# Node rows loaded before the branch, layer 1's weights prepared in the experts' stage, and its entry done tile by tile

## The chip, the cores and the metric

The kernel runs on one core of a Trainium2 chip. The metric is the device time of one execution in microseconds (us), as the median of several runs. The engines of the core are TensorE (PE; its weight loads are shown apart as PEld), VectorE (DVE), ScalarE (ACT), GpSimd (POOL) and SyncE (SP). SP, ScalarE and GpSimd issue DMAs here; GpSimd issues the indirect ones, which fetch one row of a table per partition.

## The reference

A graph of N = 3125 nodes with D = 256 features and E = 50000 edges sorted by their target goes through two layers, each with a graph part, a mixer over all nodes and a feed-forward part of 8 experts. Everything is float32. Cut to its outline:

```python
xn = layernorm(x)
x = x + gnn0(xn, edges, edge_attr) + mixer0(xn)   # edge attention with 4 heads; 4 blocks of linear attention and an MLP
x = x + experts_top2(layernorm(x))                # each node goes to 2 of 8 experts, 256-512-256 with gelu
xn = layernorm(x)
x = x + gnn1(xn, edges) + mixer1(xn)              # layer 1
x = x + experts_all(layernorm(x))                 # all 8 experts, weighted by a softmax router
```

Of layer 1 the change touches the entry and the keys and values:

```python
# gnn1: mean of the neighbours' rows, then [xn, mean] @ weight, each row divided by its norm, plus bias
# mixer1:
k, v = split(xn @ w_qkv + b_qkv)                  # 8 heads of 32
k = layernorm(k) * kln_g + kln_b                  # within a head
v = layernorm(v) * vln_g + vln_b
kv = sum over nodes of k^T v / N                  # one 32 x 32 context per head
h = gelu((q @ kv + xn) @ w1 + b1)
mixer1 = h @ w2 + b2 + xn
```

## The kernel before

`gps_kernel` (L116) turns the list of targets into columns (`edge_columns`, L155), compares them with the windows that the kernel was laid out for, reads the resulting flag into a register and branches: `fast_path` (L188) if the edges lie inside the windows, else `general_path`, which does not run here. The nodes stand in 25 tiles of Q = 128 rows (NT = 25, the last with 53), in one SBUF tensor X that is updated in place. The edges stand in 391 blocks of 128.

Layer 0 begins in `fast_path`. SP issues six loads of X (L369, groups of five tiles), then the source list, then the weights of the graph part (L373 to L383); the table loop (L384 to L397) normalises each tile (`ln_stats` L255, `normed` L267), transposes it (`transposed` L270), multiplies it (`product` L277) and stores the rows that the edge gathers read. `mixer` (L530) begins with statistics of the already normed rows (`stats_of`, L532), one pair of VectorE instructions for each tile. Edge work and mixer work are interleaved by a planner that compares costs and due times. `dispatch` (L794) routes each node to two experts and scatters its row to the `tok` table.

The experts' stage (L893 to L1012) runs 32 tiles of 256 rows. For each, SP loads rows and weights three tiles ahead (`load(k + 3)`), TensorE does two products with a Gelu on ScalarE between them, and the result is stored to the table `yex` by ScalarE's queue. Behind tile 8, 11, 14 and so on SP also loads the weights of layer 1's experts.

Then comes layer 1. Its weights are loaded and prepared at L1025 to L1050: six loads on SP, six rows spread over the partitions on ScalarE's queue, the mean of each head taken out of the key and value weights on VectorE, the query weight transposed. The entry loop (L1053 to L1079) goes through chunks of four tiles: `yex` rows are gathered (two for each tile, GpSimd) and added to X with their gates (L1064), the rows are normed by VectorE (L268), transposed into xT, multiplied by the node half of the graph weight and stored into the table `xtab`, from which the edge gathers of layer 1 read. The normed rows and the bias are then added to X:

```python
        nc.vector.tensor_tensor(xs, xs, xn[:, 0:n, :], ALU.add)
        nc.vector.tensor_tensor(xs, xs, bc(gb, 1, n), ALU.add)
```

After the entry, `other()` runs `mixer1` (L1101) and then `experts` (L1193), whose steps yield an estimate of their time; a loop (L1305 to L1315) puts a group of eight edge blocks (`sum_group`, L1270) in whenever enough of that time has been spent:

```python
    spent, g, PACE, FROM = 0.0, 0, 11.5, 14.0
        while g < len(GROUPS) and (step is None or spent >= FROM + PACE * g):
```

A group's rows are fetched by GpSimd into one of three buffers `gt1`, three groups ahead. `mixer1` takes one step for each tile for keys and values: product (two inputs of 512 columns), bias and norm within a head, then scale and shift by lng and lnb over the whole tile (L1118, L1119), then two context products that add up in PSUM over all 25 tiles; each such step yields 3.7. With the context closed, it is folded into the first MLP weight, and the MLP runs over groups of tiles from the top (`BACK`, L1098: six groups of four and a last one of tile 0 alone). `experts` takes the same groups: a group's router (`route`, L1167) and experts run when its edge sums are all in and `aggregate` (L1235) has added them to X. In PSUM there are the kinds "seg", "tr", "mm" and "acc" with two buffers each. The order of instructions on an engine follows the order of the program; where the loops above put a step decides what it queues behind.

## Time and profile before

| what | value |
|---|---|
| median of three runs | 2773.26 us (2771.87 to 2775.46) |
| profiled execution | 2773.55 us |
| its span | 2771.8 us |
| granted TensorE clock, mean | 0.968 |
| PE busy | 2596.2 us (94%) |
| PEld busy | 1875.5 us (68%) |
| DVE busy | 1523.5 us (55%) |
| ACT busy | 870.6 us (31%) |
| POOL busy | 932.1 us (34%) |
| moved by DMA | 215.84 MB |

The profile is of one execution; its span runs from the first to the last instruction. A row of digits cuts the span into 40 slices of 69.3 us; a digit is the busy share in tenths, and PEclk is the granted clock of TensorE in tenths. A window line gives a stretch, then the engines' busy time in it with the number of instructions. A line of the chain gives start, length, and the engine, PSUM kind and source line. "L280" is the product helper, so that products are told apart by the name of what they write.

### The profile page before, as it was taken

What the parts mean: (1) busy time and instruction counts of PE and PEld (TensorE: products, weight loads), DVE (VectorE), ACT (ScalarE), POOL (GpSimd) and SP (SyncE); (2) the same over time, 40 slices, a digit from 0 to 9 for tenths busy, and PEclk for the clock granted to TensorE, in tenths of its full rate; (3) what the DMA queues carried; (4) which work ended last, traced back from release to release, by engine and by line L of the source; (5) the groups of instructions that cost most, each with busy time, mean ns of one, the idle gap of its engine ahead of it and who ended that gap; (6) DMA issues with size and microseconds to landing.
All of it is one profiled execution on the core that took longest, in us unless ns stands there. A gap on an engine that the chain in (4) does not pass through costs nothing.

```text
span 2771.8 us, 29883 instructions
## 1 busy us (share of the span) xinstructions
PE 2596.2 (94%) x10578; PEld 1875.5 (68%) x10578; DVE 1523.5 (55%) x3754; ACT 870.6 (31%) x1619; POOL 932.1 (34%) x962
## 2 busy tenths in 40 slices
PE   5989999899898999898998899678899999999998
PEld 4866778667677667685666788545666666666655
DVE  6576666866668777678654311389644333232211
ACT  3432235322253222533332222232333232222233
POOL 1208552154531544200222000267555454545100
PEclk9999999999999999999997899889999999999999
DMA  4103331032212131101210886443222222222000
GB/s 146 24 14 94 86 107 30 21 90 77 88 53 75 43 87 37 56 3 38 63 51 34 263 268 209 156 121 93 67 71 76 70 69 74 82 65 77 19 8 11
DMA packets 152337, 215.84 MB, mean 78 GB/s; under 512 B 21033, under 2 KB 120687, under 8 KB 152179
## 3 DMA queue, kind: packets, MB, share of 16 engines
q1 hardware_dynamic: 104274, 112.31, 12.7%
q0 software_dynamic: 36848, 91.34, 12.0%
q10 hardware_dynamic: 11056, 10.19, 1.1%
q8 instruction: 86, 1.41, 0.2%
q14 instruction: 73, 0.59, 0.1%
HBM read 160.14 MB, written 53.61 MB: 77 GB/s over the span
## 4 chain that ended last, share of the span: by engine, by line
PE 83%; DVE 10%; ACT 2%; DMA 2%; issue 2%; POOL 1%; SPq 0%; DVEq 0%; ACTq 0%; POOLq 0%
PE mm L280 35%; PE acc L280 26%; PE seg L467 6%; PE seg L1280 6%; PE acc L614 3%; PE tr L274 3%; PE acc L335 1%; POOL gt L283 1%; PE seg L280 1%; DVE gt L422 1%; DVE kv L1116 1%; DMA ye<-yex,slot 1%; PE tr L280 1%; PE tr L982 1%; DVE kv L1118 0%
## 5 line engine op out<-in xcount | busy, mean ns | idle before, releaser
L283 POOL DMA_INDIRECT gt<-table,srcI x391 | 439.3, 1124 | 690.3 <-DVE m L425 496.5
L283 POOL DMA_INDIRECT gt<-xtab,srcI x391 | 385.2, 985 | 351.5 <-PE seg L1280 205.6
L280 PE MATMUL mm<-hT,w 128*128 128x512 f32 (+2 forms) x896 | 372.6, 555 | 10.1 <-ACT gT L690 8.6
L280 PE MATMUL acc<-w,gT 128*128 128x256 f32 x1600 | 366.8, 384 | 0.0
L280 PEld LDWEIGHTS acc<-w,gT 128*128 128x128 f32 x1600 | 302.5, 192 | 45.1 <-issue 2.5
L1221 ACT ACTIVATE fh<-mm,bn_b,bn_s 128x512 f32<-128x512 f32 (+1 forms) x224 | 163.1, 731 | 431.7 <-PE mm L280 431.7
L339 DVE SCALAR_TENSOR_TENSOR X<-acc,rw,X 128x256 f32<-128x256 f32 x200 | 95.2, 483 | 324.8 <-PE acc L280 324.5
L280 PEld LDWEIGHTS mm<-hT,w 128*128 128x128 f32 x896 | 164.1, 192 | 142.9 <-issue 93.7
L690 ACT ACTIVATE gT<-mm,cols 128x512 f32<-128x512 f32 (+2 forms) x224 | 142.2, 641 | 352.1 <-PE mm L280 351.7
L280 PE MATMUL mm<-wqkv,hT 128*128 128x256 f32 x800 | 210.0, 393 | 9.2 <-ACT K L566 6.3
L280 PE MATMUL acc<-fw_f_Wo,fh 128*128 128x256 f32 x800 | 198.1, 385 | 1.0
L280 PE MATMUL mm<-fh,fw_f_W 128*128 128x512 f32 (+1 forms) x448 | 197.0, 569 | 1.6 <-ACT fh L1221 1.3
L280 PE MATMUL mm<-xc,fw_f_W 128*128 128x512 f32 (+1 forms) x448 | 189.3, 552 | 0.0
L467 PE MATMUL seg<-vals,oh 128*128 128x261 f32 x782 | 184.0, 387 | 3.7 <-DVE vals L457 3.7
L1280 PE MATMUL seg<-gt,oh 128*128 128x256 f32 x782 | 184.3, 385 | 0.0
L280 PEld LDWEIGHTS acc<-fw_f_Wo,fh 128*128 128x128 f32 x800 | 144.7, 190 | 58.1 <-issue 18.5
L467 PEld LDWEIGHTS seg<-vals,oh 128*128 128x128 f32 x782 | 147.8, 191 | 38.0 <-DVE oh L290 5.4
L1280 PEld LDWEIGHTS seg<-gt,oh 128*128 128x128 f32 x782 | 149.5, 193 | 33.3 <-issue 13.0
L280 PEld LDWEIGHTS mm<-wqkv,hT 128*128 128x128 f32 x800 | 142.5, 195 | 32.7 <-ACT K L566 10.7
L280 PEld LDWEIGHTS mm<-fh,fw_f_W 128*128 128x128 f32 x448 | 78.8, 192 | 100.7 <-issue 65.4
L1059 POOL DMA_INDIRECT ye<-yex,slot x50 | 52.2, 1044 | 264.1 <-DVE bn_b L1092 249.2
L701 DVE TENSOR_TENSOR X<-acc,X 128x256 f32<-128x256 f32 x100 | 42.2, 422 | 151.9 <-PE acc L280 151.7
(333 smaller groups left out, 3864.5 us busy)
## 6 DMA issues: line engine op xcount, KB each, us to landing
ew<-in_e_W SPq DMA_DIRECT2D x64, 512.0 KB, 6.9
tok<-zero SPq DMA_DIRECT2D x8, 3328.0 KB, 12.7
w<-in_W SPq DMA_DIRECT2D x8, 1024.0 KB
hr<-tok SPq DMA_DIRECT2D x32, 256.0 KB, 4.7
yex<-yo ACTq DMA_DIRECT2D x32, 256.0 KB, 5.0
gt<-table,srcI POOLq DMA_INDIRECT x391, 2.6
gt<-xtab,srcI POOLq DMA_INDIRECT x391, 2.7
fw_f_W<-in_f_W SPq DMA_DIRECT2D x16, 256.0 KB, 4.0
```

Source lines behind the costliest of these rows:

```text
L274: nc.tensor.transpose(pt[:, k, :], src_row[:, k * Q:(k + 1) * Q], ident)
L280: nc.tensor.matmul(pm, a, b, start=(k == 0), stop=(k == len(lhs) - 1))
L283: nc.gpsimd.indirect_dma_start(out=dst, out_offset=None, in_=tab[:, :], in_offset=bass.IndirectOffsetOnAxis(ap=srcI[:, b:b + 1], axis=0))
L335: nc.tensor.matmul(py, cT[:, j, :], bt, start=True, stop=True)
L339: nc.vector.scalar_tensor_tensor(X[:, t, :], py, cw, X[:, t, :], op0=ALU.mult, op1=ALU.add)
L467: nc.tensor.matmul(open_seg[w_], oh[:, b - h0, :], v[:, b - h0, :], start=(b == a), stop=(b == z))
L614: nc.tensor.matmul(cx[a], K[0:r, t, a * 128:(a + 1) * 128], keys.hn[0:r, t, :], start=(t == 0), stop=(t == NT - 1))
L690: nc.scalar.activation(gT[:, f, :], pm, AF.Gelu, bias=col("b1", l * NF + f))
L701: nc.vector.tensor_tensor(X[:, t, :], py, X[:, t, :], ALU.add)
L1059: nc.gpsimd.indirect_dma_start(out=ye[0:r, j, :], out_offset=None, in_=yex[:, :], in_offset=bass.IndirectOffsetOnAxis(ap=slot[0:r, k, t0 + ...
L1221: nc.scalar.activation(hn[:, a, 0:w], pm, AF.Relu, bias=bn[s][1][:, c:c + 1], scale=bn[s][0][:, c:c + 1])
L1280: nc.tensor.matmul(segs[w], oh[:, j, :], gt[:, j, :], start=(b == z), stop=(b == a))
```

## The change

X is allocated ahead of the branch, and its six loads go onto SP directly behind the load of the target list; `node_dma` becomes a function of the module. The statistics that open `mixer` are taken from those of the table loop, as variance times the squared factor of the norm, with a mean of zero.

A generator `layer1_weights` loads and prepares layer 1's weights in five parts, called behind tiles 9, 12, 15, 18 and 21 of the experts' stage. New in it are four masks `cf` made of lng and lnb: the scale and shift of keys and values are no longer done on the rows, but on the finished context. For that a column of ones is kept beside each 128 of the normed keys and values, the context products get 129 columns, and one more product with a matrix of ones gives column sums of 258 columns, held in a "seg" buffer over all tiles.

The entry is rewritten tile by tile. Rows are fetched by `fetch_y` in groups of 2, 3, 4, 4, 4, 4 and 4 tiles into the three `gt1` buffers; `add_y` adds them and takes statistics four tiles ahead; `norm_y` writes the normed row on ScalarE and, in place of adding it, scales X by one plus the factor; `product_y` is the node product and its store. Steps of `keys_values` are put between the tiles, about three for four tiles; those left over (of 28) run in `mixer1` and yield 2.5 each. The bias add moves to `mixer1`'s loop over `BACK`, whose groups become four of four and three of three tiles. The expert norms are computed behind the entry.

```diff
+    X = pre.tile([Q, NT, D], F32, name="X", tag="X")
...
+        nc.gpsimd.memset(X[:, NT - 1, :], 0.0)
+        for t0, n in TG:
+            node_dma(nc.sync, X[:, t0:t0 + n, :], i["x"], t0, n)
...
-        fast_path(tc, i, out, ident, dstP)
+        fast_path(tc, i, out, ident, dstP, X)
...
-            for t0, n in TG:
-                node_dma(nc.sync, X[:, t0:t0 + n, :], i["x"], t0, n)
...
+                v = mv1[:, t0:t0 + n, 1]
+                nc.vector.tensor_tensor(v, mv[:, 0:n, 1], rs[:, 0:n], ALU.mult)
+                nc.vector.tensor_tensor(v, v, rs[:, 0:n], ALU.mult)
...
-            for t in range(NT):
-                stats_of(mv1, t)
...
+    def layer1_weights():
+
+        w = {}
+        w["qkv"] = weights("m_wqkv", 3 * D)
+        w["kvb"] = row_load(lp, "kv_b")
+        lng = row_load(lp, "kvln_g").rearrange("p (s d) -> p s d", s=2)
+        lnb = row_load(lp, "kvln_b").rearrange("p (s d) -> p s d", s=2)
+        yield w
+        w["1"] = weights("m_w1", D)
+        w["2"] = weights("m_w2", D)
+        w["gb"] = row_load(lp, "g_bias")
+        mb2 = row_load(lp, "m_b2")
+        w["br"] = row_load(lp, "br")
+        yield w
+        w["g"] = weights("g_w", D, 2 * KC)
+        w["r"] = weights("f_Wr", NE)
+        w["fbo"] = lp.tile([NE, D], F32, name="fbo", tag="fbo")
+        nc.sync.dma_start(w["fbo"], i["f_bo"])
+
+        hm = lp.tile([Q, KC + 1, 2 * NH], F32, name="hm", tag="hm")
+        for k in range(KC + 1):
+            v = (w["qkv"][:, k, D:3 * D] if k < KC else w["kvb"]).rearrange("p (h d) -> p h d", d=DH)
+            nc.vector.tensor_reduce(hm[:, k, :], v, AX.X, ALU.add)
+            nc.vector.tensor_scalar(hm[:, k, :], hm[:, k, :], 1.0 / DH, None, op0=ALU.mult)
+            nc.vector.tensor_tensor(v, v, bc(hm[:, k, :], 2, DH), ALU.subtract)
+        yield w
+        nc.vector.tensor_tensor(w["gb"], w["gb"], mb2, ALU.add)
+
+        w["qT"] = lp.tile([Q, KC, D], F32, name="wqT", tag="wqT")
+        for k in range(KC):
+            pt = transposed(w["qkv"][:, k, 0:D])
+            nc.vector.tensor_copy(w["qT"][:, :, k * Q:(k + 1) * Q], pt)
+        yield w
+
+
+        four = lp.tile([Q, 2, Q], F32, name="four", tag="four")
+        vc = lp.tile([Q, 2], F32, name="vcol", tag="vcol")
+        for s, row in enumerate((lng, lnb)):
+            nc.vector.tensor_copy(four[:, s, :].rearrange("p (h d) -> p h d", d=DH), bc(row[:, 1, :], 1, Q // DH))
+            pt = ps("tr", [Q, Q])
+            nc.tensor.transpose(pt, four[:, s, :], ident)
+            nc.vector.tensor_copy(vc[:, s:s + 1], pt[:, 0:1])
+        w["cf"] = lp.tile([Q, 4, Q], F32, name="cf", tag="cf")
+        nc.vector.memset(w["cf"], 0.0)
+        for s in range(2):
+            for j in range(Q // DH):
+                r = slice(j * DH, (j + 1) * DH)
+                nc.vector.tensor_scalar(w["cf"][r, 2 * s, r], (lng, lnb)[s][r, 0, :], 1.0 / N, None, op0=ALU.mult)
+            nc.vector.tensor_scalar(w["cf"][:, 2 * s + 1, :], w["cf"][:, 2 * s, :], vc[:, 1:2], float((1, N)[s]),
+                                    op0=ALU.mult, op1=ALU.mult)
+            nc.vector.tensor_scalar(w["cf"][:, 2 * s, :], w["cf"][:, 2 * s, :], vc[:, 0:1], None, op0=ALU.mult)
+        yield w
+
+    l1w, ready = None, layer1_weights()
...
+            if k >= 9 and k % 3 == 0:
+                l1w = next(ready, l1w)
...
-    BACK = [list(range(t, max(-1, t - 4), -1)) for t in range(NT - 1, -1, -4)]
+    BACK = [list(range(t, t - 4, -1)) for t in range(NT - 1, 8, -4)] + [list(range(t, t - 3, -1)) for t in (8, 5, 2)]
...
-        for j in range(n):
-            normed(xn[:, j, :], xs[:, j, :], mv, rs, j)
...
-        nc.vector.tensor_tensor(xs, xs, xn[:, 0:n, :], ALU.add)
-        nc.vector.tensor_tensor(xs, xs, bc(gb, 1, n), ALU.add)
...
+    ENT = [(0, 2), (2, 3)] + [(t, 4) for t in range(5, NT, 4)]
...
+    def fetch_y(g):
+        if g < len(ENT):
+            t0, n = ENT[g]
+            yes[g] = wk.tile([Q, 8, D], F32, name="ye", tag="gt1", bufs=3)
             for j in range(n):
                 r = rows(t0 + j)
+                for k in range(2):
+                    nc.gpsimd.indirect_dma_start(
+                        out=yes[g][0:r, 2 * j + k, :], out_offset=None, in_=yex[:, :],
+                        in_offset=bass.IndirectOffsetOnAxis(ap=slot[0:r, k, t0 + j:t0 + j + 1], axis=0))
+
+    def add_y(t):
+
+        g = ENT_OF[t]
+        t0, n = ENT[g]
+        r = rows(t)
+        for k in range(2):
+            nc.vector.scalar_tensor_tensor(X[0:r, t, :], yes[g][0:r, 2 * (t - t0) + k, :], gate[0:r, k, t:t + 1],
+                                           X[0:r, t, :], op0=ALU.mult, op1=ALU.add)
+        st = stat.tile([Q, 6], F32, name="st", tag="st", bufs=4)
+        nc.vector.bn_stats(st, X[:, t, :])
+        nc.vector.bn_aggr(mvx[:, t, :], st)
+        if t == t0 + n - 1:
+            a, b, c = (rsx[:, k, t0:t0 + n] for k in range(3))
+            nc.scalar.activation(a, mvx[:, t0:t0 + n, 1], AF.Sqrt, bias=eps5)
+            nc.vector.reciprocal(a, a)
+            nc.vector.scalar_tensor_tensor(b, mvx[:, t0:t0 + n, 0], -1.0, a, op0=ALU.mult, op1=ALU.mult)
+            nc.vector.tensor_scalar(c, a, 1.0, None, op0=ALU.add)
+            fetch_y(g + 3)
+
+    def norm_y(t):
+
+        xn = wk.tile([Q, D], F32, name="xn", tag="h", bufs=2)
+        nc.scalar.activation(xn, X[:, t, :], AF.Identity, scale=rsx[:, 0, t:t + 1], bias=rsx[:, 1, t:t + 1])
+        pt = transposed(xn)
+        nc.scalar.copy(xT[:, :, t, :], pt)
+        nc.scalar.activation(X[:, t, :], X[:, t, :], AF.Identity, scale=rsx[:, 2, t:t + 1], bias=rsx[:, 1, t:t + 1])
+
+    def product_y(t):
+        t0, n = ENT[ENT_OF[t]]
+        if t == t0:
+            yts[t0] = c4("yt").rearrange("p a (b c) -> p (a b) c", c=D)
+        py = ps("seg", [Q, D])
+        product(py, [xT[:, k, t, :] for k in range(KC)], [l1w["g"][:, KC + k, :] for k in range(KC)])
+        nc.scalar.copy(yts[t0][:, t - t0, :], py)
+        if t == t0 + n - 1:
+            nc.sync.dma_start(xtab[t0 * Q:(t0 + n) * Q, :].rearrange("(t p) c -> p t c", p=Q), yts.pop(t0)[:, 0:n, :])
+
+    def keys_values():
+
+        cx = [ps("acc", [Q, Q + 1]) for _ in range(2)]
+        ks = ps("seg", [Q, 2, Q + 1])
+
+        def sums(t):
+            kv, r = kvs[t % 3], rows(t)
+            se = dict(start=(t == 0), stop=(t == NT - 1))
+            for a in range(2):
+                nc.tensor.matmul(cx[a], kv[0:r, 2 + a, 0:Q], kv[0:r, a, :], **se)
+            nc.tensor.matmul(ks.rearrange("p a c -> p (a c)"), ones[0:r, :], kv[0:r, 0:2, :].rearrange("p a c -> p (a c)"),
+                             **se)
+
+        for t in range(NT + 2):
+            if t < NT:
+                pm = ps("mm", [Q, 2 * D])
+                product(pm, [xT[:, k, t, :] for k in range(KC)], [l1w["qkv"][:, k, D:3 * D] for k in range(KC)])
+                ks_ = c4("kv").rearrange("p s (h d) -> p s h d", d=DH)
+                kv, sq = ks_[:, 0], ks_[:, 1]
+                nc.vector.tensor_tensor(kv.rearrange("p h d -> p (h d)"), pm, l1w["kvb"], ALU.add)
+                nc.scalar.activation(sq, kv, AF.Square)
+                va = wk.tile([Q, 2 * NH], F32, name="va", tag="va")
+                nc.vector.tensor_reduce(va, sq, AX.X, ALU.add)
+                nc.scalar.activation(va, va, AF.Sqrt, bias=eps5, scale=1.0 / DH)
+                nc.vector.reciprocal(va, va)
+                nc.vector.tensor_tensor(kvs[t % 3][:, :, 0:Q].rearrange("p g (h d) -> p g h d", d=DH),
+                                        kv.rearrange("p (g h) d -> p g h d", g=4),
+                                        bc(va, 2, DH).rearrange("p (g h) d -> p g h d", g=4), ALU.mult)
+            if t >= 2:
+                sums(t - 2)
+            yield
+        cb = lp.tile([Q, 2, Q], F32, name="cb1", tag="four")
+        c2 = lp.tile([Q, Q], F32, name="cb2", tag="cb2")
+        sv = lp.tile([Q, 2], F32, name="sumv", tag="sumv")
+        cf = l1w["cf"]
+        for a in range(2):
+            nc.vector.tensor_copy(sv[:, a:a + 1], cx[a][:, Q:Q + 1])
+            nc.vector.tensor_tensor(cb[:, a, :], cx[a][:, 0:Q], cf[:, 0, :], ALU.mult)
+            nc.vector.scalar_tensor_tensor(cb[:, a, :], cf[:, 2, :], sv[:, a:a + 1], cb[:, a, :],
+                                           op0=ALU.mult, op1=ALU.add)
+            nc.vector.tensor_tensor(c2, ks[:, a, 0:Q], cf[:, 1, :], ALU.mult)
+            nc.vector.tensor_tensor(cb[:, a, :], cb[:, a, :], c2, ALU.add)
+            nc.vector.tensor_tensor(cb[:, a, :], cb[:, a, :], cf[:, 3, :], ALU.add)
+        contexts.append(cb)
...
+    contexts = []
+    for g in range(3):
+        fetch_y(g)
+    AHEAD = 4
+    for t in range(AHEAD):
+        add_y(t)
+    norm_y(0)
+    kvsteps, due = keys_values(), 0
+    for t in range(NT):
+        if t + AHEAD < NT:
+            add_y(t + AHEAD)
+        if t + 1 < NT:
+            norm_y(t + 1)
+        product_y(t)
+        while due < 0.75 * t - 0.5:
+            next(kvsteps)
+            due += 1
+    norms_of_experts()
...
-            nc.vector.tensor_tensor(k4, k4, bc(lng, 2, NH), ALU.mult)
-            nc.vector.tensor_tensor(k4, k4, bc(lnb, 2, NH), ALU.add)
...
-            yield 3.7
...
+        for _ in kvsteps:
+            yield 2.5
+        cb = contexts[0]
...
+            nc.vector.tensor_tensor(X[:, t0:t0 + n, :], X[:, t0:t0 + n, :], bc(l1w["gb"], 1, n), ALU.add)
...
```

## The prediction

> **What bounds the kernel now.** I read the slices first, then windows by stage, then the waits and the chain of the one stretch that stands out. The slices of the page:
>
> ```profile
> PE   5989999899898999898998899678899999999998
> PEclk9999999999999999999997899889999999999999
> DMA  4103331032212131101210886443222222222000
> ```
>
> TensorE is at 9 or 10 tenths nearly everywhere, so only its gaps and its own work count. The gaps are slice 1, slices 22 to 23 and slices 26 to 29. The windows (PE, PEld, DVE, ACT, POOL busy; granted clock; DMA share; GB/s) say how large the last is:
>
> ```profile
> 1540.00:1773.70 233.70, 233.67 (x1137) 203.59 (x1136) 45.41 (x70) 59.62 (x126) 0.00 (x0) 1.00 0.72 229
> 1600.00:1640.00 40.00, 40.00 (x197) 34.95 (x196) 7.60 (x11) 10.40 (x22) 0.00 (x0) 1.00 0.92 298
> 1773.70:1957.90 184.20, 127.57 (x433) 82.93 (x433) 157.45 (x349) 48.29 (x120) 110.54 (x106) 0.82 0.36 108
> 2000.00:2200.00 200.00, 198.06 (x724) 131.48 (x723) 83.40 (x195) 64.25 (x105) 105.11 (x108) 0.98 0.26 74
> ```
>
> The experts' stage (first row) is all TensorE, with VectorE and ScalarE mostly free. Layer 1's entry and its keys and values (third row) are VectorE's: 157 of 184 us, TensorE at clock 0.82. From 2000 TensorE rules again. In the chain TensorE's own pace is plain:
>
> ```profile
> 2419.05 4.29 PE mm L280 x10
> 2430.78 3.45 PE seg L1280 x16
> ```
>
> A 512-column instruction takes 0.429 us, one of 256 columns 0.2156, so one of 128 about 0.108. At this pace the third row's work is: keys and values products 100 x 0.429 = 42.9, node products 100 x 0.2156 = 21.6, contexts 100 x 0.108 = 10.8, edge sums 66 x 0.2156 = 14.2, aggregates 2.6, transposes 54 x 0.108 = 5.8: 98 us. The stretch lasts 184.2, so **86 us are lost there**: the pot. Its waits (who, for whom: us, times, longest) and two lines of the time line:
>
> ```profile
> PE tr L274 <- DVE xn L268: 26.3, 6, 11.6
> PE acc L1122 <- DVE kv L1119: 15.9, 10, 3.6
> DVE X L1064 <- DMA ye<-yex,slot: 8.3, 5, 6.2
> 1784.63 0.88 DVE L1064 SCALAR_TENSOR_TENSOR X<-ye,gate,X 128x256 f32<-128x256 f32 x2 [6.23 <-DMA ye<-yex,slot]
> 1859.96 1.46 POOL L283 DMA_INDIRECT gt<-xtab,srcI  x1 [15.43 <-DMA xtab<-yt]
> ```
>
> First TensorE waits for VectorE's normed rows, then for its normed keys and values; the edge gathers begin at 1860. The start shows in the chain:
>
> ```profile
> 10.13 4.81 DMA X<-in_x
> ...
> 17.01 10.01 DMA raw<-in_src
> ...
> 30.64 4.90 PE mm L280 x20
> ```
>
> The table's product waits until 30.6 for what SP issues behind the node rows.
>
> **The change, part by part.** The sum is made against the profiled run, 2773.55 us (its span 2771.8); the runs' median is 2773.26, the same for this purpose.
>
> *Node rows ahead of the branch.* Six loads on SP, 6.84 us of issue, move from 10.13 to about 1.3. SP sat there 7.9 us waiting for the flag, so the issue fits into that wait. They are put behind the dst load on SP and beside ScalarE's three small dst loads; should these land later the flag slips, at most about 1 us. Src, attention and table weights then meet DMA queues that are nearly empty of rows: they should come some 8.8 us earlier (10.13 - 1.3), and with them the product of 30.6, the table, the first gathers and layer 0, which has no slack. Bounds: 0, if something else gates the product, and -10; if the branch waits for outstanding loads (no row shows it), rows still come ahead of weights and about 5 stays. Taken: **-8.5**.
>
> *First statistics from the table's* (50 VectorE instructions, 25 x (0.38 + 0.16) = 13.5 us, between 39.8 and 52.1). They end at 52.1; the first normed row runs at 57.86, after the table's store. Nothing.
>
> *Weights in the experts' stage.* Six SP loads and six broadcast rows on ScalarE's queue, about 2.4 MB, go past the experts' own loads. VectorE gets 3 x (0.68 + 0.17 + 0.68) for the means and about 4 us more, beside 45 busy of 234. TensorE gets six transposes, 0.65 us, in a row with no idle. ScalarE's issues cost 0.47 us each (they did at 1777) ahead of a Gelu; TensorE has two "mm" buffers and waits for Gelu at once: at most 6 x 0.47 = 2.8. Here a rule speaks against the change: the Trainium skill, "DMA: Bandwidth & Descriptors", Specifications, gives some 358 GB/s of HBM bandwidth to a core. The row 1600 to 1640 already moves 298 at share 0.92. By the rule 60 are free and 2.4 MB need 40 us, which is hidden; if they all stood ahead of expert weights, 2.4 MB / 298 GB/s = 8 us. From 1640 the trace moves about 210 only, so I take nothing for bandwidth and **+3** in all (0 to 10).
>
> *Entry.* Removed from VectorE: two affine passes over keys and values (16.8 + 17.2), the residual adds (7.4 + 0.4; the bias add of 7.7 goes to the later feed-forward, where VectorE is 40% busy), the normed rows (9.2, to ScalarE), the weight preparation (5), the experts' norms (1.5). Left on VectorE up to the context: rows' sums and statistics 25 x (0.85 + 0.38 + 0.16) + 7 x 0.5 = 38; keys and values 16.6 + 16.5 + 6.1 + 17.0 = 56; context 3; six one-hots and five bucket sums 10: 107. The first sum no longer stands beside 2 MB of weights: gather at 1777.4, 1.56 to issue, landing as in the later gathers 2.6 after the issue began: 1780.5. In 1790 to 1850 VectorE was busy 87 to 100%; at 92% the 107 take 117: end at **1897**.
>
> TensorE: four gathers at 1.25, landing, sums, statistics, norm: first product about 1788. Work to the context 42.9 + 21.6 + 10.8 + 5.4, two groups' sums 6.9, aggregates 1.7, and new: the column sums, 50 instructions of 258 columns, **10.9**. Together 100: 1888 at best, so VectorE ends last. ScalarE: two normalising passes at 0.51 (its scaled copy L1240), two copies at 0.37, and (0.63 + 0.31) for keys and values: 2.7 x 25 = 68, hidden. POOL: 50 row gathers at 1.25 end at 1840; last row, product and store put the edge gathers at 1856 to 1866, as now. With folding the context and G about 5 us are bare: TensorE is saturated from 1902. Of 128.3 us since 1773.7 it worked 103.5; lost 25 instead of 86. Gain 86 - 25 - 10.9 = **-50**.
>
> A second rule: column sums hold one of the two "seg" buffers, so each node product waits for ScalarE's copy of the one before. The Trainium skill, "TensorE: Matmul & The Clock Gate", section on psum-queue depth-cycling, warns that micro-idles between matmul groups let the clock fall to half. By it, 100 us of work at the 0.83 of 1810 to 1840 would take 120, end 1908, gain 39. But those rows have TensorE busy only 6.4 of 10; now 2.6 us of keys-and-values work stands ready between two products, while a copy takes 0.37. I keep -50 and put 39 in the range.
>
> *Node order at the end.* The one-tile group ran 29.1 us (2737.3 to 2766.4) for 20.7 of work; a three-tile group should lose about 0.5 per expert, like a four-tile one: -4.4. But mixer units shrink from 25 x 3.7 to 10 x 2.5, so the last edge group (due at 14 + 48 x 11.5 = 566) comes just before the last tiles' experts (at 570), and their router can't be issued ahead: aggregate 4.1 + router 2.7, less 3 of other work; the last store is three tiles, +0.9. **+1** net (-4 to +6).
>
> Sum: 2773.5 - 8.5 + 3 - 50 + 1 = **2719**.
>
> **Rivals.** *A, half the pot* (0.22): keys and values are pushed behind the entry by its own VectorE work. Entry to 1852, then 56 + 3 + 16 at 92% = 82: 1934 instead of 1952, and the column sums are hidden: some -26. 2773.5 - 8.5 + 3 - 26 + 1 = 2743. For it: VectorE is at 9.4 to 10 from 1790 to 1820. Against: 25 us less of it per entry.
>
> *B, slower* (0.07): the waits that now stand at 1781, where ScalarE waits 10.2 us for a row load and TensorE 9.2 for a weight, move into the queues of the experts' stage and stop TensorE. Five points at 10.2 are 51; from 55 us on it decides: 2719 + 58 = 2777. Against: loads land in about 5 us there.
>
> *C, the rows bring nothing* (0.10): the branch drains them and the flag waits: 2728.
>
> *D, both engines full from 1790* (0.11): VectorE at 100% and keys and values all inside the entry: 1888, lost 15: 2706.
>
> **How the numbers follow.** The main case has 0.50, A 0.22, D 0.11, C 0.10, B 0.07. The range takes D and most of A, and the unknown bounds (experts' stage 0 to 10, clock 11): 2698 to 2745. Main, A, D and C are faster by over 0.2% (5.5 us, about what a measurement tells): 0.93. Of B, 0.03 only eats the gain up and stays within; 0.04 goes beyond: slower.
>
> **What would show it.** Table product at about 22 instead of 30.6; experts' stage 234 to 240 us long; first row sum at 1780.5 on the old clock (shifted by the start); VectorE about 107 busy to the context, which is closed about 123 us after the experts' end instead of 178; edge gathers still some 85 us after it; the last sums close to the last tiles' router. Wrong it would be if TensorE showed idle in the experts' stage, if VectorE stayed the last to end well after 1910, or if POOL made edge groups wait.

## The result, and the profile after

The changed kernel takes **2738.54 us** (median of four runs, 2737.68 to 2742.77) against 2772.57 for the kernel before (four runs): a ratio of 0.9878, 95% interval 0.9861 to 0.9896, so 34 us less. The forecast was 2719 with a range of 2698 to 2745: the direction and the range hold, but of the 54 us that were forecast 34 came. The profiled execution has a span of 2737.1 us at a mean clock of 0.975.

The slices of the page of the changed kernel (40 of 68.4 us):

```profile
PE   6989999899899999998998799969999999999998
PEclk9999999999999999999999799989999999999999
DMA  5003331032312131100111786542222222222200
```

Of the gap of slices 26 to 29 one slice is left, the 27th, with 6 tenths; slice 1 has risen from 5 to 6.

Windows by stage (columns as before: PE, PEld, DVE, ACT, POOL busy; granted clock; DMA share; GB/s). First the kernel before, from the end of the experts' stage to the first MLP product of layer 1, and ten microseconds near its beginning:

```profile
1773.70:1977.00 203.30, 146.49 (x523) 99.32 (x523) 173.28 (x390) 53.95 (x136) 121.37 (x117) 0.84 0.35 104
1780.00:1790.00 10.00, 1.08 (x4) 0.71 (x4) 5.37 (x14) 1.79 (x3) 7.56 (x9) 0.50 1.00 320
```

Then the changed kernel: its experts' stage, the same stretch behind it, and the beginning of that stretch in tens:

```profile
1541.72:1775.20 233.48, 231.58 (x1127) 201.37 (x1125) 46.83 (x79) 59.08 (x125) 0.00 (x0) 1.00 0.71 229
1775.20:1918.35 143.15, 111.30 (x462) 74.64 (x461) 103.08 (x257) 67.22 (x165) 76.77 (x76) 0.90 0.31 92
1780.00:1790.00 10.00, 0.00 (x0) 0.00 (x0) 3.89 (x11) 0.29 (x1) 7.56 (x9) 0.50 0.32 92
1790.00:1800.00 10.00, 3.25 (x8) 1.74 (x8) 4.73 (x16) 2.80 (x7) 7.57 (x9) 0.50 0.37 107
1800.00:1810.00 10.00, 7.92 (x25) 5.24 (x26) 6.57 (x24) 4.75 (x11) 7.56 (x9) 0.69 0.44 131
```

The stretch lasts 143 us instead of 203, with VectorE busy 103 instead of 173. What is left is its front. TensorE was nearly idle there before too (its first transposed row came 21.9 us behind the stage, now 19.9), but then it waited for a weight, and VectorE was full from 1790. Now TensorE does nothing at all from 1780 to 1790, and VectorE is not the reason by its load (39 and 47%). The waits of the changed kernel from 1770 to 2000 (who, for whom: us, times, longest), and from its time line the first product of the table and the first edge gathers of the two layers:

```profile
POOL gt L288 <- DVE va L1190: 40.0, 2, 39.7
...
PE tr L279 <- ACT xn L1153: 24.3, 3, 19.9
...
DVE X L1137 <- DMA ye<-yex,slot: 20.2, 23, 2.7
...
PE seg L285 <- ACT yt L1164: 5.6, 3, 3.4
```

```profile
23.33 2.18 PE L285 MATMUL mm<-wcat,xt 128*128 128x136 f32 x8
...
53.17 1.12 POOL L288 DMA_INDIRECT gt<-table,srcI  x1 [40.85 <-DVE hn L722]
...
1884.65 0.96 POOL L288 DMA_INDIRECT gt<-xtab,srcI  x1 [39.72 <-DVE va L1190]
```

TensorE's waits for keys and values (15.9 us before) are gone, and of those for normed rows one long one is left, 19.9 us. The product of the table comes 7.3 us earlier, layer 1's edge gathers 24.7 us later. The name in their wait (`va`) misleads: what they need is the last rows of `xtab`, whose product ended at 1880.3 and whose store was issued at 1880.7.

For the sum by stages, each TensorE instruction is counted at full pace (columns x 0.429 / 512 us, at least 0.108), and what a stretch lasts beyond that is called lost: idle time and slow clock together.

| stretch | before: length, lost | after: length, lost |
|---|---|---|
| start to the first output product of the experts' stage | 1542.4, 198.3 | 1541.7, 196.8 |
| experts' stage | 231.3, 2.1 | 233.5, 4.5 |
| its end to the first MLP product | 203.3, 87.2 | 143.1, 39.7 |
| from there to the end | 794.8, 49.9 | 818.7, 50.8 |

Behind the experts' stage the work at full pace went from 861.0 to 871.3 us. So the 34.7 us of the two spans are: start -0.7, experts' stage +2.2, lost time of the entry -47.4, work added +10.3, lost time behind it +0.9. These are one profile of each kernel. In the repeat of the changed kernel below, the entry lost 42.5 and the rest 54.9, so a term is known to some 4 us.

### The profile page after: what moved, and what is told of

It is laid out like the page before. It is cut to its first block, busy times and chain, and to the rows that moved or that the text cites. A ratio compares the mean times of both kernels' runs of the same rounds, so it can differ in the third digit from the quotient of the medians.

```text
span 2737.1 us, 29869 instructions
## 1 busy us (share of the span) xinstructions
PE 2581.4 (94%) x10630; PEld 1879.5 (69%) x10630; DVE 1475.2 (54%) x3670; ACT 892.3 (33%) x1668; POOL 934.7 (34%) x962
## 5 line engine op out<-in xcount | busy, mean ns | idle before, releaser
L285 PE MATMUL mm<-hT,w 128*128 128x512 f32 (+2 forms) x896 | 374.2, 557 | 10.3 <-ACT gT L694 8.8
L1388 PEld LDWEIGHTS seg<-gt,oh 128*128 128x128 f32 x782 | 147.6, 190 | 32.8 <-issue 11.5
L285 PEld LDWEIGHTS mm<-wqkv,hT 128*128 128x128 f32 x800 | 143.2, 196 | 33.2 <-ACT K L570 10.9
L285 PEld LDWEIGHTS mm<-xc,fw_f_W 128*128 128x128 f32 x448 | 85.9, 192 | 58.5 <-issue 40.5
```

What stands on the lines that cost most here:

```text
L285: nc.tensor.matmul(pm, a, b, start=(k == 0), stop=(k == len(lhs) - 1))
L1388: nc.tensor.matmul(segs[w], oh[:, j, :], gt[:, j, :], start=(b == z), stop=(b == a))
```

## The experiments

The experiments ran on three chips. On the first the kernel before takes 2772 us, on the two others 2952 and 2949. There TensorE, VectorE and ScalarE stand still together again and again, often with no wait that the profile shows (the last section has the numbers). Each run is therefore compared with others of its chip, and small differences on the slower chips stay open.

**The changed kernel again**, beside three of the other runs on the faster chip:

> The changed kernel once more, unchanged, as the measure for the others on this chip: its ratio to the kernel before should be near 0.988.

2744.74 us, ratio 0.9894 (0.9877 to 0.9910). Its MLP begins 145.9 us behind the experts' stage (143.1 in the first profile).

**The order on VectorE.** In the changed kernel the front of the entry reads like this in the time line (start, length, engine, line, operation, tiles; in brackets the idle time before it and what ended it):

```profile
1782.46 0.48 DVE L1137 SCALAR_TENSOR_TENSOR X<-ye,gate,X 128x256 f32<-128x256 f32 x1 [2.67 <-DMA ye<-yex,slot]
...
1789.36 0.29 ACT L1144 ACTIVATE rsx<-mvx,eps 128x2 f32<-128x2 f32 x1 [11.69 <-DVE mvx L1141]
...
1791.33 0.48 DVE L1137 SCALAR_TENSOR_TENSOR X<-ye,gate,X 128x256 f32<-128x256 f32 x1 [0.54 <-DMA ye<-yex,slot]
...
1792.57 0.48 DVE L1137 SCALAR_TENSOR_TENSOR X<-ye,gate,X 128x256 f32<-128x256 f32 x1 [0.67 <-DMA ye<-yex,slot]
...
1793.31 0.15 DVE L1145 RECIPROCAL rsx<-rsx 128x2 f32<-128x2 f32 x1
...
1794.46 1.09 ACT L1153 ACTIVATE xn<-X,rsx 128x256 f32<-128x256 f32 x2 [4.80 <-DVE mvx L1141]
...
1795.12 1.18 PE L279 MATMUL tr<-ident,xn 128*128 128x128 f32 x4 [19.89 <-ACT xn L1153]
```

ScalarE has the root of the first group's variances ready at 1789.65. The reciprocal that makes the factor of it needs 0.15 us, but on VectorE it stands behind row sums of later tiles, which wait for their gathered rows; it runs at 1793.31. The statistics that the root needs stood behind such sums too. The program text does not show this order: in it `add_y(1)` finishes the first group's factors before `add_y(2)` begins its sums. The statement ahead of the prediction that an engine follows the order of the program does not hold here; the order has to be read from the trace. The edit puts the sums of a group behind the factors of the group before:

```diff
+    ready_of = {}
+
+    @contextmanager
+    def behind(g):
+
+        with ExitStack() as s:
+            if g in ready_of:
+                s.enter_context(tc.issue_after(ready_of[g]))
+            yield
+
...
         for k in range(2):
-            nc.vector.scalar_tensor_tensor(X[0:r, t, :], yes[g][0:r, 2 * (t - t0) + k, :], gate[0:r, k, t:t + 1],
-                                           X[0:r, t, :], op0=ALU.mult, op1=ALU.add)
+            with behind(g - 1):
+                nc.vector.scalar_tensor_tensor(X[0:r, t, :], yes[g][0:r, 2 * (t - t0) + k, :], gate[0:r, k, t:t + 1],
+                                               X[0:r, t, :], op0=ALU.mult, op1=ALU.add)
...
             nc.vector.tensor_scalar(c, a, 1.0, None, op0=ALU.add)
+            ready_of[g] = next(x for x in reversed(nc.cur_bb.bb.instructions) if x.engine == nc.vector.engine)
```

> On VectorE the row sums of a group of tiles are put behind the norm factors of the group before; nothing else is changed. Theory: in the changed kernel the factors of the first group were ready to be finished at 1789.7, but stood behind two sums that waited for gathered rows until 1793.3 (and the second group's from 1796.5 to 1800.9); without that TensorE starts some 4 us earlier and its next gap of 3.7 us goes too: 4 to 8 us faster than the changed kernel. Rival: the rows come at 2.5 us a tile and set the pace anyway: within 1.5 us.

2729.56 us (2728.69 to 2734.14), ratio 0.9847 (0.9830 to 0.9863): 15 us less than the changed kernel on the same chip, about twice what was expected. Its time line:

```profile
1785.13 0.29 ACT L1155 ACTIVATE rsx<-mvx,eps 128x2 f32<-128x2 f32 x1 [9.86 <-DVE mvx L1152]
1785.46 0.17 DVE L1156 RECIPROCAL rsx<-rsx 128x2 f32<-128x2 f32 x1 [0.36 <-ACT rsx L1155]
...
1786.63 1.18 PE L279 MATMUL tr<-ident,xn 128*128 128x128 f32 x4 [13.80 <-ACT xn L1165]
```

TensorE begins 13.8 us behind the stage instead of 19.9: 1.8 us of this are the root, 3.6 the wait of the reciprocal behind it. The same wait of the second and third group, 4.4 and 2.9 us in the changed kernel, is 0.0 and 0.6 here. A third gap, of the changed kernel's waits above, hangs on the same queue over one engine more:

```profile
1848.55 0.48 DVE L1137 SCALAR_TENSOR_TENSOR X<-ye,gate,X 53x256 f32<-53x256 f32 x1 [2.27 <-DMA ye<-yex,slot]
...
1851.21 0.63 ACT L1188 ACTIVATE kv<-kv 128x512 f32<-128x512 f32 x1 [3.52 <-DVE kv L1187]
1851.75 0.35 ACT L1164 COPY yt<-seg 128x256 f32<-128x256 f32 x1
...
1852.15 1.13 PE L285 MATMUL seg<-w_g_w,xnT 128*128 128x256 f32 x4 [3.43 <-ACT yt L1164]
```

VectorE's row sum waits for a row, the keys and values queue behind it, ScalarE's square waits for these, its copy of a node product queues behind the square, and TensorE waits for the buffer that the copy frees. Waits of this kind (5.7 us in the copy of the changed kernel) are gone with the new order. In all, the idle time of the stretch is 20.6 us instead of 32.6, the lost time 27.4 instead of 42.5, and the MLP begins 130.8 us behind the stage instead of 145.9. The step is shown.

**Weights.** Leaving out the calls in the experts' stage and running the generator behind it:

```diff
-            if k >= 9 and k % 3 == 0:
-                l1w = next(ready, l1w)
...
+    for l1w in ready:
+        pass
```

> All five parts of the weight preparation run behind the experts' stage, all else as in the changed kernel. The experts' stage gets its 2.2 us back. Theory one: the loads and the 5 us of VectorE work fit beside the wait for the first rows, since TensorE starts only 20 us behind the stage anyway: 2737 to 2741. Theory two (the prediction's): the first row sum slips again from 7.3 to about 11 us behind the stage and VectorE has 5 us more at the front: 2742 to 2748.

2921.66 us on a slower chip, ratio 0.9901. The run doesn't test what it was made for: the loads, and the means taken from the weights, were drawn into the experts' stage all the same (the first weight is loaded 70 us into it), since their buffers were free. A second kernel gives them a pool that opens only when the experts' buffers are released:

```diff
+    lp2 = ctx.enter_context(tc.tile_pool(name="lp2", bufs=1))
...
-        t = lp.tile([Q, k, n], F32, name=f"w_{name}", tag=f"w_{name}")
+        t = lp2.tile([Q, k, n], F32, name=f"w_{name}", tag=f"w_{name}")
...
+    for l1w in layer1_weights():
+        pass
```

> The weights and rows of layer 1 get a pool of their own that is opened only when the experts' buffers are free, so that their loads and preparation can't start before the experts' stage has ended (in the run before, the same edit without a new pool left the loads in the stage). The experts' stage should be 1.9 us shorter. Theory one (the trace): the first row sum stands at 7.2 us and the first node product at 21 us behind the stage, mostly on the wait for gathered rows, so the loads fit beside it: within 3 us of the changed kernel. Theory two (the prediction): the first sum slips to about 11 us and VectorE gets 5 us more work at the front: 5 to 10 us slower than the changed kernel.

2740.11 us, ratio 0.9878 (0.9861 to 0.9895), not told apart from the changed kernel's 0.9894. The delays of theory two are all there: in its time line TensorE waits for a weight, VectorE prepares weights between the first sums, and the first transposed row comes 27.1 us behind the stage.

```profile
1775.74 1.09 PE L279 MATMUL tr<-ident,w_m_wqkv 128*128 128x128 f32 x4 [9.42 <-DMA w_m_w<-in_m_w]
...
1778.43 0.50 DVE L1138 SCALAR_TENSOR_TENSOR X<-ye,gate,X 128x256 f32<-128x256 f32 x1 [7.39 <-DMA ye<-yex,slot]
...
1793.44 0.69 PE L279 MATMUL tr<-ident,xn 128*128 128x128 f32 x2 [8.89 <-ACT xn L1154]
```

Yet its MLP begins 145.8 us behind the stage, as in the unchanged copy (145.9). While it starts late, GpSimd goes on gathering, so the rows are there when TensorE comes, and of the later gaps most are gone. Theory two had the delay right and its cost wrong: the delay is real, and it is made up. As the entry stood, the place of the weights made no difference to it; whether it does with the better order of the run above wasn't tried. Ahead of the entry there is a difference: the experts' stage is 231.3 us long, as in the kernel before (232.8 in the copy), and it begins 5.8 us earlier than in the copy; the part on the rows comes back to this.

**Steps of keys and values out of the entry**:

```diff
-        while due < 0.75 * t - 0.5:
-            next(kvsteps)
-            due += 1
```

> No step of keys and values is put into the entry by the program; all 28 follow behind it. Theory one: the interleaving carries the gain. The rows come at 2.5 us a tile (two gathers of 1.25), so the entry ends near 85 us behind the experts' stage, then 25 steps of 2.6 follow: the context is closed 150 us behind the stage instead of 132, 10 to 20 us slower: 2748 to 2758. Theory two: the steps are drawn into the entry anyway, as they were before the change (keys-and-values products stood at 1801 there): within 3 us of 2738.

2942.93 us, ratio 0.9969, 21 us more than the run with late weights on the same chip (which stands in for the changed kernel here: it differs only in where the weights are called for). The context is closed 203 us behind the stage instead of 182. Theory one, and a little more than it said: the interleaving carries some 21 us. Its price is seen too: without it the edge gathers begin 107 us behind the stage, with it 138 on that chip.

**Column sums** for the last tile only; this kernel leaves the other 24 out, so its contexts are not right and only its time is of use:

```diff
-            nc.tensor.matmul(ks.rearrange("p a c -> p (a c)"), ones[0:r, :], kv[0:r, 0:2, :].rearrange("p a c -> p (a c)"),
-                             **se)
+            if t == NT - 1:
+                nc.tensor.matmul(ks.rearrange("p a c -> p (a c)"), ones[0:r, :],
+                                 kv[0:r, 0:2, :].rearrange("p a c -> p (a c)"), start=True, stop=True)
```

> The column sums of keys and values are made for the last tile only (the other 24 are left out, so the context misses their part); the rest is as in the changed kernel. The prediction's step: the 258-column products stand on TensorE, 24 x 0.44 = 10.5 us faster. Rival: TensorE's 2.60 us a step falls to 2.16, but VectorE needs 2.27 a step and 3.2 a tile inside the entry, so VectorE takes the pace over: 3 to 6 us faster.

2736.99 us, 7.8 less than the changed kernel on that chip. The MLP begins 135.9 us behind the stage, 10.0 earlier: the prediction's 10.5, on TensorE's account. The waits inside change, but cancel:

```profile
PE acc L1177 <- DVE kvs L1194: 4.5, 4, 2.7
```

These waits for normed keys show VectorE as the next bound (0.8 us in the copy), and the 5.7 us of waits for the node products' buffers are not there. The rest of the run lost 4 us more than in the copy, within what profiles of the same code differ by.

**Rows behind the branch again**, on both slower chips:

```diff
-        for t0, n in TG:
-            node_dma(nc.sync, X[:, t0:t0 + n, :], i["x"], t0, n)
...
             tmp = s.enter_context(tc.tile_pool(name="t0", bufs=1))
+            for t0, n in TG:
+                node_dma(nc.sync, X[:, t0:t0 + n, :], i["x"], t0, n)
```

> The six loads of the node rows go back behind the branch, all else as in the changed kernel. From the trace: the table product comes about 7 us later again (near 30 instead of 23.3), but of this lead only 0.7 us was left at the first product of the experts' stage, so the run is 0 to 2 us slower than the changed kernel, about 2739 to 2741. The prediction's step (rows ahead of the branch are worth 8.5): 2745 to 2748.

> The kernel of the first experiment (row loads behind the branch) once more, since the stalls on the chip of that run hid small differences. The changed kernel's ratio to the kernel before was 0.988 and 0.9894. Theory one (the lead is lost on the way to the experts' stage): 0.988 to 0.9905. Theory two (the lead of 5 to 7 us at the first gather arrives): 0.991 to 0.9925.

2927.09 (ratio 0.9921, 0.9895 to 0.9947) and 2926.39 us (0.9918, 0.9892 to 0.9944). By the ratio alone theory two looks better, but the changed kernel itself wasn't run on these chips, and the intervals reach over both. The profiles say more: with the loads behind, the first edge gather comes at 58.0 and 58.5 us, in the six other runs of these chips at 51.9 to 53.9, so the lead there is 6; at the first output product of the experts' stage the two stand at 1672.1 and 1674.7, the six at 1669.0 to 1673.2, mean 1671.2. Of 6 us some 2 arrive there. Where the rest can go is seen in the profiles of the faster chip, in two lines of the same four products, before and after:

```profile
1179.74 1.03 PE L280 MATMUL mm<-wqkv,hT 128*128 128x256 f32 x4
```

```profile
1175.16 1.91 PE L285 MATMUL mm<-wqkv,hT 128*128 128x256 f32 x4
```

The same instruction of TensorE comes 5.0 us earlier than before at 79 us, 4.8 at 1174, 3.2 at 1209 and 1.8 at 1308. The two steps are two spells of 3.4 us in which the clock stands at half where it stood at full before, one here and one at 1277. At the first transposes of the experts' stage 1.6 us are left (0.7 at its first output product, ahead of which eight transposes more stand than before). The copy and the runs with the order and without the column sums have both spells and lose the same 1.7 and 1.6 us. But the run with the weights behind, which issues its rows ahead of the branch like these, has neither. Its lead is 6.8 us at 79 and 7.4 at the experts' stage: it arrives whole. The first transposes of that stage before, in the changed kernel, and in that run:

```profile
1533.63 1.08 PE L982 MATMUL tr<-ident,hr 128*128 128x128 f32 x4 [10.95 <-DVE upto L917]
```

```profile
1532.02 1.09 PE L1049 MATMUL tr<-ident,hr 128*128 128x128 f32 x4 [11.16 <-DMA hr<-tok]
```

```profile
1526.23 1.09 PE L990 MATMUL tr<-ident,hr 128*128 128x128 f32 x4 [11.00 <-DVE upto L925]
```

Ahead of the first spell TensorE stands idle for 2.45 us in all these profiles, with the spell behind it or not, so the idle time alone does not decide it. What does isn't shown, nor whether the place of the weights has to do with it: each kernel has one profile, and the run with the rows behind on the first of the slower chips has neither spell, with its weights in the stage.

**Pace of the edge groups**, 10.5 units for each instead of 11.5:

```diff
-    spent, g, PACE, FROM = 0.0, 0, 11.5, 14.0
+    spent, g, PACE, FROM = 0.0, 0, 10.5, 14.0
```

> The edge groups are due every 10.5 units instead of 11.5, all else as in the changed kernel. Theory: the last edge group came so late (2648) that the last three tiles' norm and router stood bare: a gap of 3.6 us, another of 0.6, and products at half clock behind it, 2 to 3 us. With the groups about 1.4 us closer each, the last comes some 60 us earlier and the router is issued ahead: 5 to 8 us faster, 2730 to 2734. Rival: the groups only move work forward and something else, the row gathers or the sums' buffers, stalls for as much: within 2 us of 2738.

2915.15 us, ratio 0.9881, against 2921.66 and 0.9901: 6.5 less, with intervals that overlap. The gap that it was to close belongs to the router of the last three tiles, which is bare: nothing is left to cover its wait. It stands in the changed kernel's time line as

```profile
2655.27 0.73 PE L279 MATMUL tr<-ident,hs 128*128 128x128 f32 x4 [3.64 <-DVE hs L273]
...
2659.10 4.68 PE L285 MATMUL mm<-xc,fw_f_W 128*128 128x384 f32 x8
```

(the second line takes 2.6 us at full clock). With the router itself, which takes 1.3 us more than its work, and a later gap of 0.6, the bare router costs 3.6 + 0.6 + 2.1 + 1.3 = 7.6 us. With the new pace the last sums stand 133 us ahead of the end instead of 89, and those gaps are not there. How much of the 7.6 shows in the time is open: the part behind the entry lost 55.5 us, against 56.8 in the run with late weights.

**Order and pace together**, and then with first groups of 1, 2 and 2 tiles:

> Both edits together: row sums behind the norm factors, and edge groups due every 10.5 units. The order alone came to a ratio of 0.9847 to the kernel before. Theory: the pace takes away the bare router of the last three tiles (3.6 + 0.6 us of gaps and 2 to 3 us of products at half clock) on top: ratio 0.982 to 0.9835, some 4 to 8 us less. Rival: what the pace saves at the end it loses earlier: 0.984 to 0.986.

```diff
-    ENT = [(0, 2), (2, 3)] + [(t, 4) for t in range(5, NT, 4)]
+    ENT = [(0, 1), (1, 2), (3, 2)] + [(t, 4) for t in range(5, NT, 4)]
```

> As the run with order and pace, and the first groups of the entry are of 1, 2 and 2 tiles instead of 2 and 3. Theory: the first norm waits for two gathered rows instead of four, 2 x 1.25 = 2.5 us earlier, and TensorE's first work with it: 2 to 3 us faster than order and pace. Rival: the rows of the tiles behind come no earlier, so TensorE only waits later: within 1 us.

2908.13 (ratio 0.9858, 0.9820 to 0.9896) and 2909.06 us (0.9864, 0.9839 to 0.9890), both on a slower chip. They are 17 to 18 us below the kernel with the rows behind, but not told apart from each other. Both medians lie where the rivals put them (0.984 to 0.986; within 1 us), yet the intervals reach over the theories too, so neither is decided. The first transposed row comes 13.8 and 11.3 us behind the stage, the 2.5 us as worked out; what they are worth in time stays open. Part of the reason is that the stalls of this chip fall into the entry. In the run with the rows behind, for instance:

```profile
1956.97 0.37 ACT L1155 COPY xnT<-tr 128x256 f32<-128x256 f32 x1 [14.55 <-remote]
...
1957.39 2.07 PE L283 MATMUL seg<-w_g_w,xnT 128*128 128x256 f32 x4 [15.16 <-issue]
```

"remote" and "issue" are what the profile writes when it shows no wait that ended.

**The old node order** in layer 1, six groups of four and tile 0 alone:

```diff
-    BACK = [list(range(t, t - 4, -1)) for t in range(NT - 1, 8, -4)] + [list(range(t, t - 3, -1)) for t in (8, 5, 2)]
+    BACK = [list(range(t, max(-1, t - 4), -1)) for t in range(NT - 1, -1, -4)]
```

> The node order of layer 1 goes back to six groups of four tiles and tile 0 alone; all else as in the changed kernel (0.988 to 0.9894 of the kernel before). The prediction's step: the short last group costs 8.4 us more than its work but its router isn't exposed: within 2 us of the changed kernel. Rival: the three-tile groups are a gain of their own and the exposed router comes from the later edge groups, whichever order: 6 to 9 us slower, 0.990 to 0.992.

2909.58 us, ratio 0.9843 (0.9816 to 0.9869). Both expectations miss: they put it at the changed kernel's ratio or above, and it lies below (the changed kernel itself wasn't run on this chip; 0.9878 and 0.9894 are from the faster one). The run with the rows behind makes the comparison clean behind the entry, since its entry on the same chip is the same (MLP at 190.5 us in both): behind the entry the old order lost 51.9 us, the new one 62.9. Of these 11 us some 7.6 would be the bare router by the sum above. It isn't there in the old order, where the last sums belong to tile 0 alone and its router is worked ahead while the four-tile group runs. With the new order and the new pace the lost time is 51.6 on this chip (55.5 in the run with the pace alone on the other), which fits. So three-tile groups seem to do no harm by themselves, but with the late edge groups they do. On this chip it is one profile each, and on the other slow chip the new order with the old pace lost 62.6 in one run and 56.8 in another.

## Why the prediction was right, and where not

The result is in the range, but the main case is not what put it there. Two terms came out short, the rows by about 8 us and the entry by 13, and the range had been drawn wide enough to take in rival A, whose mechanism did not happen either; the repeat's 2744.74 is at its very edge. That part of it is luck.

- **Rows ahead of the branch, -8.5: measured -0.7 at the experts' stage** (-0.6 to -2.8 in the three other profiles with the weights in that stage, -7.4 in the run with the weights behind). The first half held: the flag slipped 0.74 us, the table product came at 23.3 (forecast 22), the first gather 5.4 us earlier. "Layer 0, which has no slack" is not refuted, since in one run the lead went through it whole. What the term left out is the clock, which could run at half in places where it hadn't: two such spells took 3.2 of the 5 us. How much arrives on average is not settled: 0.6 to 7.4 us by the profiles, 0 to 7 by the times.
- **First statistics, 0.** TensorE's wait for the first normed rows is 4.0 us, 3.6 before, so nothing came of it that shows; not tried alone.
- **Weights in the experts' stage, +3: measured +2.2** (+3.1 from the stage's first transposes on), by the mechanism named: VectorE stood for the landing of the key and value weight ahead of the copy that ScalarE's store waits for, and the Gelu behind that store came 1.87 us late for TensorE, as the time line of the changed kernel shows:

```profile
1553.39 1.28 DVE L928 TENSOR_REDUCE hm<-w_m_wqkv 128x16 f32<-128x512 f32 x2 [3.54 <-DMA w_m_wqkv<-in_m_wqkv]
...
1555.40 0.68 DVE L1071 COPY yo<-acc 128x512 f32<-128x512 f32 x1
...
1556.11 0.38 ACTq L1072 DMA_DIRECT2D yex<-yo  x1
...
1557.06 1.13 PE L285 MATMUL mm<-hTe,ew 128*128 128x256 f32 x4 [1.87 <-ACT egT L1063]
```

  Rival B's mechanism is thus real, once and for 1.9 us instead of five times for 10.2. It was not the bandwidth: the stage's DMA share is 0.71 as before. With the weights behind, the stage took its 231.3 us again. The means above were made in the stage's first 15 us, although the calls stand behind tile 9 and later in the program: here too the engine's order was not the program's.
- **Entry, lost 86 to 25: measured 87.2 to 39.7** (42.5 in the repeat). This is the large miss, 13 us. The failed step is "four gathers at 1.25, landing, sums, statistics, norm: first product about 1788", 14.3 us behind the stage. The sum came as forecast (7.2 us behind the stage, forecast 6.8), but the product at 21.1. The times of the parts were right and the order of the queue was not: what is ready waits behind what is not, on an engine that is half idle. With the order mended the product comes at 15.0 and the loss is 27.4, near the 25 of the forecast.
- **Column sums, +10.9: measured +10.3** by the work added and 10.0 by leaving them out.
- **Node order and end, +1: measured +0.9 in the first profile, but +5.0 in the repeat**, and +5.9 to +9.0 in the three other runs of that chip, whose code behind the entry is the same. So the net is not shown to be right. The prediction named the bare router, and why: the units shrink, so the edge groups fall due late. It put it too low: it costs about 7.6 where aggregate and router less other work were put at 3.8, since it and the products behind it ran in part at half clock. The old order lost 11 us less behind the entry on the slower chip. What the shorter last group is worth, put at -4.4, wasn't measured alone.
- **The rule against the change.** The Trainium skill, "TensorE: Matmul & The Clock Gate", section on psum-queue depth-cycling, warns of micro-idles between groups of matmuls that let the clock fall to half. By the prediction's estimate from it the gain would have been 39 instead of 50. In the trace no such cycling shows: from 1810 to 1890 the clock is 1.00, although TensorE did wait for ScalarE's copies there, 5.6 us in three waits. In this stretch and behind it, the half clock is that behind the long gaps, at 1780 to 1804 and behind the bare router. By the stages the entry brought 37.1 (47.4 - 10.3), close to the rule's number for another reason.
- **Signs.** VectorE was busy 103 us to the MLP, forecast 107 to the context. First row sum, end of the experts' stage (233.5 us, forecast 234 to 240) and the late last sums came as said. Two did not: the context was closed 131 us behind the stage, not 123, and the edge gathers began 109 us behind it, not 85, since the steps put between the tiles hold the last node product back (17 of the 25 products for keys and values stand ahead of it, 2 before). The late gathers weren't foreseen, but they are not what bares the router at the end. With the better order and without the column sums the gathers began 97 and 100 us behind the stage, and the last sums still came 92 us ahead of the end (89 and 90 in the changed kernel and its copy), with the same gap of 3.6 us. It is the due times: with the new pace, and also where all steps of keys and values count towards them (the run without steps in the entry), the last sums came 130 to 133 us ahead and the gap was gone.
- **The rivals.** The time lies near A's 2743, but A's reason (VectorE pushes keys and values behind the entry) is not what happened: they ran inside it, and VectorE was busy 103 of 143 us. C's (the branch drains the rows) is not either. Two of the rivals' times do not follow from their working: B adds 58 where its working gives 51, and D's loss, 10 less than the main case's, makes 2709 and not 2706. Neither matters for the result.

On the faster chip the fastest kernel is the one with the mended order: 2729.56 us, 0.9847 of the kernel before. The one with the old node order has 0.9843 on its chip, not told apart from it; the two together weren't tried.

## What to carry to other kernels

When an engine works through a queue in order, cost a new stage by what stands ahead of each short instruction in that queue, not by the engine's load: here 0.15 us of VectorE held TensorE for 4 us, and the mend was worth 15. Read that order from a trace, not from the program text. A lead gained early in a long kernel has to be compared at several points on its way before it is counted: here it shrank in two places by the clock alone in some runs and in none of them in another. Where due times are counted in units of other work, and some of that work moves elsewhere, set the due times again, or the gain of one end is paid at the other.

## What had not been expected of the hardware

The same kernel takes 2772 us on one chip and 2949 to 2952 on two others, 6.4% more, at a mean clock of about 0.945 instead of 0.97. Only part of that is the clock: between the changed kernel's first profile and that of the run with the rows behind, TensorE's busy time grows by 49 us (2581.4 to 2630.3), the span by 193. Part of the rest are stretches in which TensorE, VectorE and ScalarE are idle together for more than 3 us: 13 of them in the slower profile, up to 14 us long and 83 us in all, against one of 3.5 us in the other. GpSimd's gathers often go on in them. Their cause stays open.
